# Layer 0 of a four-layer convolution kernel: twelve operations to GpSimd, line sums made once, another set-up order, and the last output by columns

## The chip, the cores and the metric

The kernel runs on one core of a Trainium2 chip. The metric is device time in microseconds, the median of three runs. The core has TensorE (PE, matrix products), VectorE (DVE), ScalarE (ACT) and GpSimd (POOL), and three queues that issue transfers here: SyncE's (SP), ScalarE's and GpSimd's. Each engine and each queue works through its own instructions in order.

## The reference

```python
x = x + L0(gn(x), core0, core1, core2)     # three cores of a tensor train: 16x16x16 -> 16x16x16
x = x + L1(gn(x), ...)                     # depthwise Sobel filters, two dense layers, masks of "alive" cells
x = x + L2(gn(x), filters, bias)           # 3x3 convolution, 16 -> 16 channels
x = x + L3(gn(x), ...)                     # like L1
```

`x` is 1024 x 16 x 16 x 16, float32. `gn` subtracts the mean and divides by the root of the variance of each of 8 groups of 2 channels. The first layer is one linear map of the 4096 values of an image, made of three small cores:

```python
for core in (core0, core1, core2):
    r, o, i, k = core.shape
    new = jnp.einsum('roik,brix->bkox', core, res.reshape(bs, r, i, -1))
```

## The kernel before

**Layer 0.** The batch is two halves of 512 images. The map of layer 0 is done as a fast block multiplication on two levels. The outer table `OUTER` has 13 entries, here called pairs (phases in the code): each names the lines of g that its matrices use (0 to 3), and which blocks of the normalized input its two operands sum. A pair has four units (one for each quarter `q` of the output), and a unit does the seven products of the inner table `INNER`, k = 0 to 6, in 14 steps of 4 matmuls of 128 x 256 (`pieces`, L1567). A 32-bit matmul leaves two records in the trace, so a step is x8 there.

The matrices are built on the fly. `g`, the product of the second and third core, is made by small matmuls (`gmul`, L644), copied by ACT and written to DRAM by `keep_g` in two layouts, `g_dram[0]` (L651) and `g_dram[1]` (L658). `early` makes its first rows (h = 0, q = 0 and 1), on POOL's queue; `piece` makes the rest, woven into the first pair, on SP's queue. `gload` brings two lines of g at a time into a tile `gq`; a third or fourth line goes into a second place (`xn` in the profile). `build` multiplies them on PE (L1459) by `R`, which `coefs` makes from the first core; four ACT copies (L1464) make the result `w`. `mix` adds or subtracts blocks of `w` on DVE: s2, s5, s1, s7, w01 (L1489, L1491). `gather` adds the products to the results on DVE and ACT (L1603 to L1613), with one input in PSUM.

**Opening.** `input_steps` loads the first 512 images in eight transfers on SP's queue. DVE takes their statistics (L1086, L1116), PE transposes the images (L1092), ACT copies them out. `root` and `newton` make the inverse deviation; `widen` and `spread` bring both statistics into the layout of the lines (`mr`), through PE and ACT. `first_normed(b, i)` normalizes a block of the first pair in four DVE operations of 128 x 1024: x00, x11, x10, x01 (L1174). `combined` makes the five operands that the products k >= 2 need (L1203). `kept` stores the raw first rows for later, on POOL's queue. The calls near the end of the program write this order out by hand; `before` lists what is woven in ahead of which step of the first pair. x01 stands ahead of step 7; the sum that needs it stands ahead of step 8, and the product on w01 (k = 5, step 10) reads that sum.

**The second pair's input.** `part_steps(1)` is spread over the first pair. It loads the first block of operand 0 and of operand 1 (two transfers each, L1232), normalizes both on DVE (8 operations each, L1174), saves them to `xb` on SP (L1238), adds block to block (L1242), and then adds from the first pair's blocks (`from_first`, L1315, L1325). The fourth load comes late, since the second unit's results `r` lie in its place until then.

**The third pair** uses the lines (0, 1, 3): `gload` fetches (0, 1) and then (1, 3), and `build` has two groups of matmuls.

**The end.** The last layer's last half of the batch is turned back by `turn`: PE transposes (ptx, L1867), DVE copies into `xo` (L156), which overlies the tile `xn`. Turns come for q = 0 to 3 and w2 = 0 to 7; the last two w2 of q = 3 are done in two half batches `hf`. Ahead of them in the queues stand loads of weights `wq`, of neighbour lines `nx` and of residuals. With (q, w2) = (3, 7) the images leave on SP's queue, in stores of 8 image rows (L1882).

Of the kernel before, what the change touches and what calls it, by code (L numbers as in the profile page):

```python
# [10 lines left out]
F32 = mybir.dt.float32  # L11
# [10 lines left out]
P = 128  # L22
NB = 512
# [82 lines left out]
def conv_preact_kernel(ctx: ExitStack, tc: tile.TileContext, a: dict, out: bass.AP):  # L106
# [97 lines left out]
    al_c = cst("al_c", [P, 2])  # L204
    V.tensor_reduce(al_c, ident.rearrange("p (m v h) -> p v m h", v=2, h=S), AX.XY, ALU.add)
    al_k = cst("al_k", [P, 8])
    KINDS = [(1, 0), (0, 1), (1, 1), (1, -1)]
# [234 lines left out]
    def conv_weights(room):  # L442
# [53 lines left out]
        dram.tile([2, 4, 2, 4, 2, S, 4 * P], F32, tag=f"g_dram{i}", name=f"g_dram{i}") for i in range(2)  # L496
    ]

    xb = {
        (b, n): dram.tile([P, 8, NB], F32, tag=f"xb{b}{n}", name=f"xb{b}{n}")  # L500
        for b in range(4)
        for n in range(NCH)
# [6 lines left out]
            (".... -... .... +...", "+30 +00 -20", "+30")),  # L509
        ((0, 1, 3), None, ("..++ ..++ .... ....", "+30", "+00 -20"),  # L510
            (".-.. .-.. .... .+++", "+10", "+30")),
# [20 lines left out]
    ]  # L532
    UNIT = [(1, 0, 0, 0), (0, 1, 0, 0), (0, 0, 1, 0), (0, 0, 0, 1)]

# [55 lines left out]
    def train_setup(room):  # L590
# [26 lines left out]
        G.memset(room[:, 0:1024], 0.0)  # L617
        for t in range(2):
            V.tensor_copy(c0r[:, t], c0n[:, t].unsqueeze(1).broadcast_to([P, 8, S]))

        def sums():

            t = st0["A"] = work([P, 2, P], "A", "A")
# [23 lines left out]

        def keep_g(h, q, g, queue):

            for w in range(2):  # L650
# [4 lines left out]
            for w in range(2):  # L655
                for v in range(2):
                    rows = slice(64 * w + 32 * v, 64 * w + 32 * v + 32)
                    queue.dma_start(  # L658
                        g_dram[1][v, q, w, :, h].rearrange("o k (t f) -> (k t) o f", t=2), g[rows]
                    )  # L660

        def early():

            g = work([P, 2, 8, P], "w0", "gw")
            pg = [bank([P, 2, 4, 64], "w", "pg") for _ in range(4)]
            for x in range(2):
                for k in range(4):
                    for r in range(4):
                        gmul(pg[r][:, x, k], 0, k % 2, x, r, k // 2)
            for q, x, r in product(range(2), range(2), range(4)):  # L670
                f = 64 * x + 16 * r
                A.copy(
                    g.rearrange("p q (o i) f -> p q i o f", i=2)[:, q, :, :, f : f + S],
                    pg[r][:, x, 2 * q : 2 * q + 2].rearrange("p i (o j) -> p i o j", j=S),
                )
                if (x, r) == (1, 3):
                    keep_g(0, q, g[:, q].rearrange("p (o i) f -> p o (i f)", i=2), G)

        def piece(q, h, r0):
# [13 lines left out]
            if r0 == 2:  # L693
                keep_g(h, q, g.rearrange("p o i f -> p o (i f)"), nc.sync)

        rest = [
# [364 lines left out]
    def input_steps(n, tag, queue):  # L1061
# [108 lines left out]

    def centre_scale(out, x, n, cols, k):

        m = mr[n][:, k, cols].unsqueeze(1).broadcast_to([P, out.shape[1], cols.stop - cols.start])
        V.tensor_tensor(out, out if k else x, m, ALU.mult if k else ALU.subtract)  # L1174

    def first_normed(b, i):

        X, E = part_tile(0)
        cols = slice(256 * i, 256 * i + 256)

        def op(t, k):
            x = X[:, b, t : t + 4, i]
            centre_scale(x, x if b else raw[:, t : t + 4, i], 0, cols, k)

        return [(1.2, lambda t=t, k=k: op(t, k)) for t in (0, 4) for k in range(2)]
# [31 lines left out]
    def part_steps(j):  # L1217
# [15 lines left out]

        def norm(x, n):
            return [(1.2, lambda k=k: centre_scale(x, x, n, full, k)) for k in range(2)]

        def save(block, wh, t, k, x):
            nc.sync.dma_start(xb[block][:, 4 * wh + t : 4 * wh + t + k], x)  # L1238

# [5 lines left out]
        loads = [(0, lambda p=p, wh=wh: load(p, wh)) for p in range(2) for wh in range(2)]  # L1245
        steps = loads[: 3 if j == 1 else 4] + [8]
        for p in range(2):
            if p == 1 and j == 1:
                steps.append(loads[3])
            if first[p] in fresh:  # L1250
                for wh, t in places:
                    steps += norm(lines(p, wh, t, 2), first[p][1])
                    if t:
                        steps.append((0, lambda p=p, wh=wh: save(first[p], wh, 0, 4, lines(p, wh))))
        left = [x[1:] for x in terms]
# [131 lines left out]
    def layer_train():  # L1387
# [34 lines left out]
        def gload(u, h, queue=nc.sync):  # L1422
# [5 lines left out]
            for at in range(0, len(lines), 2):  # L1428
# [6 lines left out]
                if len(pair) == 1:  # L1435
                    pair = (pair[0] - 2, pair[0]) if pair[0] in (2, 3) else (pair[0], pair[0] + 2)
                if pair[1] - pair[0] == 2:
                    queue.dma_start(g, g_dram[0][pair[0], q, h].rearrange("o s k f -> (o s k) f"))
# [35 lines left out]
        def mix(u, what):  # L1474
# [9 lines left out]
            )[what]  # L1484
            into = block(u, 0, 1)
            x, y = block(u, *x), block(u, *y)
            if out:
                t = st[what, u] = work([P, 2, 4, P], out, what)
                V.tensor_tensor(t.rearrange("p s t m -> p (s t m)"), x, y, f)  # L1489
            else:  # L1490
                V.tensor_tensor(into, x, y, f)  # L1491

# [53 lines left out]
        def pieces(u, k):  # L1546
# [176 lines left out]
    def layer_nca(X, n, l, L, xo=None):  # L1723
# [139 lines left out]
        def turn(q, w2, r, hf):  # L1863
# [6 lines left out]
            for v in range(2):  # L1870
# [6 lines left out]
                )  # L1877
            if (q, w2) == (3, 7):
                for h in range(0, S, 8):
                    for g in range(g0, g0 + n):  # L1880
                        b0 = NB + g * P
                        nc.sync.dma_start(  # L1882
                            out[b0 : b0 + P, h : h + 8].rearrange("b h w c -> b (h w c)"),
                            xo[:, g, h : h + 8].rearrange("p h w c -> p (h w c)"),
                        )

# [3 lines left out]

        later = []

# [147 lines left out]
    with ExitStack() as es:  # L2040
# [19 lines left out]
        build(0, 1)  # L2060
        build(0, 0)
        now(stat[1] + tail[:2])
        mix(0, "s2")
        now([spread0] + tail[2:] + [spread1])
        x00, x11, x10, x01 = (first_normed(*at) for at in ((0, 0), (1, 1), (1, 0), (0, 1)))
        now(x00[0::2] + x00[1::2])
        mix(0, "s5")
# [7 lines left out]
            5: more[4:6],  # L2075
            7: x01,
            8: more[6:8],
# [11 lines left out]
        def sums_late(j):  # L2089
            c = combined(j)  # L2090
            woven_into(j, {2 * k + 1: c[2 * k : 2 * k + 2] for k in range(5)})

        late = range(1, NP)
        woven_into(0, before)
# [11 lines left out]
        for i in range(4):  # L2106
# [8 lines left out]
            6: (fold1, 0.92),  # L2115
            7: (set3, 0.85),
            8: (conv_weights(rooms[1]), 0.9),
# [84 lines left out]
```

## Time and profile before

| | us |
|---|---|
| median of three runs (2741.51 to 2749.51) | 2746.04 |
| profiled execution, its own time | 2746.07 |
| its span, first to last instruction | 2744.3 |
| PE busy | 2675.8 (98%) |
| DVE busy | 1994.9 (73%) |
| ACT busy | 1241.4 (45%) |
| POOL busy | 541.3 (20%) |

The first pair's products run from 47 to 183 us of the span, the second pair's from 186 to 313, the third pair's from 313 to 428 (its builds from 295 to 395), and layer 0's last ends near 1560. A line of the profile names the program line, the engine, the operation, the tile written and the tiles read. [...] Buffer numbers are left out of names, so `xn` is either of the two large tiles.

### The profile page before, as it was taken

What the parts mean: (1) busy time and instruction counts of PE and PEld (TensorE: products, weight loads), DVE (VectorE), ACT (ScalarE), POOL (GpSimd) and SP (SyncE); (2) the same over time, 40 slices, a digit from 0 to 9 for tenths busy, and PEclk for the clock granted to TensorE, in tenths of its full rate; (3) what the DMA queues carried; (4) which work ended last, traced back from release to release, by engine and by line L of the source; (5) the groups of instructions that cost most, each with busy time, mean ns of one, the idle gap of its engine ahead of it and who ended that gap; (6) DMA issues with size and microseconds to landing.
All of it is one profiled execution on the core that took longest, in us unless ns stands there. A gap on an engine that the chain in (4) does not pass through costs nothing.

```text
span 2744.3 us, 47734 instructions
## 1 busy us (share of the span) xinstructions
PE 2675.8 (98%) x19246; PEld 1756.9 (64%) x19246; DVE 1994.9 (73%) x2416; ACT 1241.4 (45%) x2091; POOL 541.3 (20%) x690
## 2 busy tenths in 40 slices
PE   6999999999999999999999999999999999999997
PEld 5888888888888878888778733333333333334344
DVE  8597667867787766667887777658778858756654
ACT  3324222222232222333332276776767756676664
POOL 2000351312122742311331111111113221110000
PEclk8999999999999999999999999999999999999998
DMA  7686788997897687889689764555575866444665
GB/s 254 215 317 227 242 169 214 236 221 188 193 242 193 154 187 180 226 229 263 171 188 257 148 165 102 108 159 122 106 195 83 202 150 143 101 89 116 180 175 209
DMA packets 264796, 502.17 MB, mean 183 GB/s; under 512 B 32804, under 2 KB 100440, under 8 KB 255360
## 3 DMA queue, kind: packets, MB, share of 16 engines
q1 hardware_dynamic: 180752, 338.78, 37.1%
q0 software_dynamic: 83632, 160.22, 33.9%
q8 instruction: 152, 2.49, 0.4%
q14 instruction: 68, 0.56, 0.1%
q10 hardware_dynamic: 192, 0.13, 0.0%
HBM read 280.66 MB, written 223.35 MB: 184 GB/s over the span
## 4 chain that ended last, share of the span: by engine, by line
PE 81%; DVE 8%; DMA 5%; issue 3%; POOL 1%; ACT 1%; SPq 0%; DVEq 0%; POOLq 0%; ACTq 0%
PE po L1567 37%; PE ph L1974 21%; PE po L1803 8%; PE po L1658 5%; PE pw L1459 4%; DMA xn<-in_x_dram 1%; PE po L1667 1%; DVE xn L1174 1%; DMA xf<-r 1%; DMA xn<-xf 1%; DVE xn L1203 1%; PE ptx L1867 1%; DMA L_conv_kp<-xn 1%; DMA xb<-xn 0%; DMA xn<-xn 0%
## 5 line engine op out<-in xcount | busy, mean ns | idle before, releaser
L1977 ACT ACTIVATE hid<-ph,pack 128x512 f32<-128x512 f32 (+1 forms) x1040 | 641.3, 684 | 313.5 <-PE ph L1974 254.3
L1567 PE MATMUL po<-xn,s 128*128 128x256 f32 x3328 | 756.7, 384 | 13.6 <-DVE s L1489 7.2
L1567 PEld LDWEIGHTS po<-xn,s 128*128 128x128 f32 x3328 | 628.5, 191 | 117.5 <-issue 16.7
L1567 PE MATMUL po<-xn,w 128*128 128x256 f32 x2496 | 565.0, 381 | 1.4 <-DVE xn L1203 1.4
L1974 PE MATMUL ph<-xn,wq 32*128 32x512 f32 (+1 forms) x3752 | 518.3, 590 | 1.9 <-DVE u L1815 1.5
L1567 PEld LDWEIGHTS po<-xn,w 128*128 128x128 f32 x2496 | 468.2, 190 | 74.1 <-issue 5.9
L1464 ACT COPY w<-pw 128x512 f32<-128x512 f32 x416 | 213.6, 600 | 454.6 <-PE pw L1459 371.8
L1974 PEld LDWEIGHTS ph<-xn,wq 32*128 32x128 f32 x3752 | 233.6, 184 | 228.9 <-issue 210.0
L1974 PE MATMUL ph<-xn,pack 32*128 32x512 f32 x1288 | 274.2, 607 | 5.6 <-DVE u L1815 1.6
L1489 DVE TENSOR_TENSOR s<-w 128x1024 f32<-128x1024 f32 x208 | 251.2, 1217 | 28.1 <-PE po L1567 24.8
L1803 PE MATMUL po<-hid,pack 128*32 128x512 f32 (+1 forms) x2080 | 256.0, 592 | 0.8 <-ACT hid L1977 0.5
L1815 DVE SCALAR_TENSOR_TENSOR u<-po,pack,xn 128x512 f32<-128x512 f32 (+1 forms) x130 | 96.3, 741 | 168.2 <-PE po L1803 167.1
L1857 POOL DMA_DIRECT2D xf<-u x96 | 82.6, 860 | 618.7 <-DVE u L1855 592.1
L754 DVE TENSOR_TENSOR xn<-xn,m 128x1024 f32<-128x1024 f32 x128 | 150.2, 1217 | 34.7 <-ACT m L777 34.6
L1974 PEld LDWEIGHTS ph<-xn,pack 32*128 32x128 f32 x1288 | 115.6, 184 | 90.7 <-issue 63.1
L1803 PEld LDWEIGHTS po<-hid,pack 128*32 128x32 f32 x2080 | 53.9, 109 | 174.9 <-ACT hid L1977 86.3
L1658 PE MATMUL po<-xn,convw 128*128 128x512 f32 x368 | 163.6, 598 | 0.0
L1203 DVE TENSOR_TENSOR xn<-xn 128x1024 f32<-128x1024 f32 x130 | 152.7, 1215 | 8.0 <-DMA L_conv_kp<-xn 8.0
L1459 PE MATMUL pw<-R,gq 32*128 32x128 f32 x3328 | 143.7, 286 | 7.5 <-DVE small L1116 6.9
L1603 DVE TENSOR_TENSOR r<-r,po 128x1024 f32<-128x1024 f32 x78 | 95.0, 1218 | 72.9 <-PE po L1567 61.0
L1459 PEld LDWEIGHTS pw<-R,gq 32*128 32x128 f32 x3328 | 116.2, 188 | 41.9 <-issue 38.6
L1541 POOL DMA_DIRECT2D xf<-xn x69 | 89.8, 1776 | 251.2 <-DVE xn L1534 71.7
(229 smaller groups left out, 2784.9 us busy)
## 6 DMA issues: line engine op xcount, KB each, us to landing
xn<-xf SPq DMA_DIRECT2D x128, 512.0 KB
xn<-xb SPq DMA_DIRECT2D x36, 1024.0 KB
wq<-L_conv_wy SPq DMA_DIRECT2D x192, 192.0 KB
xf<-xn POOLq DMA_DIRECT2D x69, 512.0 KB, 10.8
piece<-xb SPq DMA_DIRECT2D x64, 512.0 KB
xf<-r POOLq DMA_DIRECT2D x48, 512.0 KB, 12.7
xf<-u POOLq DMA_DIRECT2D x96, 256.0 KB, 4.2
gq<-g_dram SPq DMA_DIRECT2D x94, 256.0 KB
```

What stands on the lines that cost most here:

```text
L754: V.tensor_tensor(part, part, m().unsqueeze(1).broadcast_to([P, 2, NB]), op)
L1203: V.tensor_tensor(out, y, z, f)
L1459: T.matmul(pw[r][:, v, i], g[rows, P * (2 * v + i) : P * (2 * v + i) + P], R[rows, k], start=k == 0, stop=k == len(gs) - 1,)
L1464: A.copy(w.rearrange("p b s t m -> p (b s t) m")[:, :, 32 * r : 32 * r + 32].rearrange("p k (v o) -> p v k o", v=2), pw[r].rearrange("p v ...
L1489: V.tensor_tensor(t.rearrange("p s t m -> p (s t m)"), x, y, f)
L1567: T.matmul(po[:, i], matrix(u, what)[:, i, t], x, start=t == 0, stop=t == 3)
L1603: V.tensor_tensor(part, part, po.unsqueeze(2).broadcast_to([P, 2, 2, 256]), ALU.add)
L1658: T.matmul(st["po", h][wh], conv["fw"][:, y], X[:, 16 * wh + h + y - 1], start=y == max(0, 1 - h), stop=y == min(2, S - h),)
L1803: T.matmul(po[32 * j : 32 * j + 32], nca["w1"][:, v], hid[j], start=v == 0, stop=v == 1)
L1815: V.scalar_tensor_tensor(u, po, nca["b1"], X[:, 8 * q + w2, cols(hf)], ALU.add, ALU.add)
L1974: T.matmul(ph, w, x, start=k == 0, stop=k == len(tiles) - 1)
L1977: A.activation(h, ph, AF.Relu, bias=nca["bt"][:, r : r + 1])
```

## The change

Six edits, all in layer 0 but the last two:

- **Set-up order.** The copies `c0r` move into `sums`, and `cores` comes ahead of `sums`; both stand after the first eight statistics. In `early`, the first quarter's writes to `g_dram[0]` are followed by the two loads `gload(0, 1)` and `gload(0, 0)`, and the writes to `g_dram[1]` come after. `build(0, 0)` moves from before the root to after the two `spread` steps. ACT, not DVE, does the widening of the mean (`widen(0)`) of the first half.
- **x01 on GpSimd.** `first_normed(0, 1, G)`: four operations, ahead of the first product in the program's order.
- **Second pair's operand 1 on GpSimd.** `part_steps(1)` takes operand 1 first: its eight normalizations and its two saves go to GpSimd and its queue. The fourth, late load is now the second half of operand 0, so the second unit's results move to column 4096.
- **Sum of two lines of g.** `piece` loads line 0 of each quarter back (tile v0, two loads on SP), DVE adds to line 1 line 0 (`scalar_tensor_tensor` with the 0-or-1 column `low`), and two stores put the sum into `g_sum`. The third pair's entry reads (4, 3), 4 standing for the sum of lines 0 and 1; `gload` takes both from `g_sum` in one load.
- **Layer 3's weights** are set up sooner within their pair (0.75 in place of 0.85).
- **Last output by columns.** With q = 3, `turn` queues columns 0 to 8 at w2 = 3, 8 to 12 at w2 = 5, 12 to 16 at w2 = 7. Each turn sends up to two of them on GpSimd's queue; the last turn sends what is left, its first on SP.

```diff
-        ((0, 1, 3), None, ("..++ ..++ .... ....", "+30", "+00 -20"),
+        ((4, 3), None, ("..++ ..++ .... ....", "+30", "+00 -20"),
...
-        def early():
+        def early(then):
...
                 if (x, r) == (1, 3):
-                    keep_g(0, q, g[:, q].rearrange("p (o i) f -> p o (i f)", i=2), G)
+                    gs = g[:, q].rearrange("p (o i) f -> p o (i f)", i=2)
+                    keep_g(0, q, gs, G, second=False)
+                    if q == 0:
+                        then()
+                        keep_g(0, q, gs, G, first=False)
+            keep_g(0, 1, gs, G, first=False)
...
         def piece(q, h, r0):
+            if h == 1 and r0 == 0:
+                st0["v0"] = t = work([P, 4, 256], "t4", "v0")
+                for w in range(2):
+                    nc.sync.dma_start(
+                        t[64 * w : 64 * w + 64],
+                        g_dram[0][0, q, w].rearrange("o s k (t f) -> (s k t) o f", t=2),
+                    )
...
+            if h == 1 and r0 == 2:
+                t = st0.pop("v0")
+                V.scalar_tensor_tensor(
+                    t, t, low, g.rearrange("p o i f -> p o (i f)"), ALU.mult, ALU.add
+                )
+                for w in range(2):
+                    nc.sync.dma_start(
+                        g_sum[q, w].rearrange("o s k (t f) -> (s k t) o f", t=2),
+                        t[64 * w : 64 * w + 64],
+                    )
...
-                V.tensor_copy(
+                (A.copy if n == k == 0 else V.tensor_copy)(
...
-    def centre_scale(out, x, n, cols, k):
+    def centre_scale(out, x, n, cols, k, on=V):
...
-        V.tensor_tensor(out, out if k else x, m, ALU.mult if k else ALU.subtract)
+        on.tensor_tensor(out, out if k else x, m, ALU.mult if k else ALU.subtract)
...
-        steps = loads[: 3 if j == 1 else 4] + [8]
-        for p in range(2):
-            if p == 1 and j == 1:
-                steps.append(loads[3])
+        steps = ([loads[0]] + loads[2:] if j == 1 else loads) + [8]
+        for p in (1, 0) if j == 1 else (0, 1):
+            on, queue = (G, G) if j == p == 1 else (V, nc.sync)
+            if j == 1 and p == 0:
+                steps.append(loads[1])
...
+                if pair == (4, 3):
+                    queue.dma_start(g, g_sum[q, h].rearrange("o s k f -> (o s k) f"))
...
-                    at = {1: (1, 6144), 3: (1, 14336)}.get(u)
+                    at = {1: (1, 4096), 3: (1, 14336)}.get(u)
...
-            if (q, w2) == (3, 7):
-                for h in range(0, S, 8):
-                    for g in range(g0, g0 + n):
...
+            if q == 3 and w2 in (3, 5, 7):
+                w = slice({3: 0, 5: 8, 7: 12}[w2], 2 * w2 + 2)
+                leave.extend((g, w) for g in range(g0, g0 + n))
+            end = (q, w2, hf) == (3, 7, 1)
+            for i in range(min(len(leave), len(leave) if end else 2)):
+                g, w = leave.pop(0)
+                b0 = NB + g * P
+                (nc.sync if end and i == 0 else G).dma_start(
+                    out[b0 : b0 + P, :, w].rearrange("b h w c -> b h (w c)"),
+                    xo[:, g, :, w].rearrange("p h w c -> p h (w c)"),
+                )
...
-        now([sums])
+        now(stat[0][:1] + [cores, sums])
         coefs(0)
-        now([cores] + stat[0])
-        early()
-        gload(0, 1, queue=G)
-        gload(0, 0, queue=G)
+        now(stat[0][1:])
+        early(lambda: (gload(0, 1, queue=G), gload(0, 0, queue=G)))
...
-        build(0, 0)
         now(stat[1] + tail[:2])
         mix(0, "s2")
-        now([spread0] + tail[2:] + [spread1])
-        x00, x11, x10, x01 = (first_normed(*at) for at in ((0, 0), (1, 1), (1, 0), (0, 1)))
-        now(x00[0::2] + x00[1::2])
+        x00, x11, x10 = (first_normed(*at) for at in ((0, 0), (1, 1), (1, 0)))
+        now([spread0] + tail[2:] + x00[:1] + [spread1])
+        build(0, 0)
+        now(x00[2:3] + x00[1:2] + x00[3:])
+        now(first_normed(0, 1, G))
...
-            7: x01,
...
-            7: (set3, 0.85),
+            7: (set3, 0.75),
```

More of the change, by code (lines that the diff above doesn't have):

```diff
@@ L205, in conv_preact_kernel @@
     V.tensor_reduce(al_c, ident.rearrange("p (m v h) -> p v m h", v=2, h=S), AX.XY, ALU.add)
+    low = cst("low", [P, 1])
     al_k = cst("al_k", [P, 8])
@@ L497, in conv_preact_kernel @@
     ]
+    g_sum = dram.tile([4, 2, 4, 2, S, 4 * P], F32, tag="g_sum", name="g_sum")
     xb = {
@@ L532, in conv_preact_kernel @@
     ]
-    UNIT = [(1, 0, 0, 0), (0, 1, 0, 0), (0, 0, 1, 0), (0, 0, 0, 1)]
+    UNIT = [(1, 0, 0, 0), (0, 1, 0, 0), (0, 0, 1, 0), (0, 0, 0, 1), (1, 1, 0, 0)]
     def read(table):
@@ L617, in train_setup @@
         G.memset(room[:, 0:1024], 0.0)
-        for t in range(2):
-            V.tensor_copy(c0r[:, t], c0n[:, t].unsqueeze(1).broadcast_to([P, 8, S]))
         def sums():
+            for t in range(2):
+                V.tensor_copy(c0r[:, t], c0n[:, t].unsqueeze(1).broadcast_to([P, 8, S]))
             t = st0["A"] = work([P, 2, P], "A", "A")
@@ L646, in gmul, with keep_g @@
             )
-        def keep_g(h, q, g, queue):
-            for w in range(2):
+        def keep_g(h, q, g, queue, first=True, second=True):
+            for w in range(2 * first):
                 queue.dma_start(
@@ L654, in keep_g @@
                 )
-            for w in range(2):
+            for w in range(2 * second):
                 for v in range(2):
@@ L1169, in input_steps, with first_normed @@
         return loads, stat, lines, tail, [lambda: spread(0), lambda: spread(1)], kept
-    def centre_scale(out, x, n, cols, k):
+    def centre_scale(out, x, n, cols, k, on=V):
         m = mr[n][:, k, cols].unsqueeze(1).broadcast_to([P, out.shape[1], cols.stop - cols.start])
-        V.tensor_tensor(out, out if k else x, m, ALU.mult if k else ALU.subtract)
-    def first_normed(b, i):
+        on.tensor_tensor(out, out if k else x, m, ALU.mult if k else ALU.subtract)
+    def first_normed(b, i, on=V):
         X, E = part_tile(0)
@@ L1182, in op @@
             x = X[:, b, t : t + 4, i]
-            centre_scale(x, x if b else raw[:, t : t + 4, i], 0, cols, k)
+            centre_scale(x, x if b else raw[:, t : t + 4, i], 0, cols, k, on)
         return [(1.2, lambda t=t, k=k: op(t, k)) for t in (0, 4) for k in range(2)]
@@ L1232, in load, with norm, save @@
             nc.sync.dma_start(lines(p, wh), source(first[p], first[p] in fresh, wh, 0, 4))
[L1234 to L1238, printed above, removed]
+        def norm(x, n, on=V):
+            return [(1.2, lambda k=k: centre_scale(x, x, n, full, k, on)) for k in range(2)]
+        def save(block, wh, t, k, x, queue=nc.sync):
+            queue.dma_start(xb[block][:, 4 * wh + t : 4 * wh + t + k], x)
         def add(p, wh, t, x, sign):
@@ L1245, in part_steps @@
         loads = [(0, lambda p=p, wh=wh: load(p, wh)) for p in range(2) for wh in range(2)]
-        steps = loads[: 3 if j == 1 else 4] + [8]
-        for p in range(2):
-            if p == 1 and j == 1:
-                steps.append(loads[3])
+        steps = ([loads[0]] + loads[2:] if j == 1 else loads) + [8]
[3 more added lines that the diff above has]
+                steps.append(loads[1])
             if first[p] in fresh:
                 for wh, t in places:
-                    steps += norm(lines(p, wh, t, 2), first[p][1])
+                    steps += norm(lines(p, wh, t, 2), first[p][1], on)
                     if t:
-                        steps.append((0, lambda p=p, wh=wh: save(first[p], wh, 0, 4, lines(p, wh))))
+                        steps.append((0, lambda p=p, wh=wh, queue=queue: save(
+                            first[p], wh, 0, 4, lines(p, wh), queue
+                        )))
         left = [x[1:] for x in terms]
@@ L1436, in gload @@
                     pair = (pair[0] - 2, pair[0]) if pair[0] in (2, 3) else (pair[0], pair[0] + 2)
-                if pair[1] - pair[0] == 2:
+                if pair == (4, 3):
+                    queue.dma_start(g, g_sum[q, h].rearrange("o s k f -> (o s k) f"))
+                elif pair[1] - pair[0] == 2:
                     queue.dma_start(g, g_dram[0][pair[0], q, h].rearrange("o s k f -> (o s k) f"))
@@ L1484, in mix @@
             )[what]
-            into = block(u, 0, 1)
             x, y = block(u, *x), block(u, *y)
@@ L1490, in mix @@
             else:
-                V.tensor_tensor(into, x, y, f)
+                V.tensor_tensor(block(u, 0, 1), x, y, f)
         def matrix(u, what):
@@ L1877, in turn @@
                 )
-            if (q, w2) == (3, 7):
-                for h in range(0, S, 8):
-                    for g in range(g0, g0 + n):
[L1881 to L1891, printed above, removed]
+            if q == 3 and w2 in (3, 5, 7):
[9 more added lines that the diff above has]
+                )
+        later, leave = [], []
         def after(n, fn):
@@ L2091, in sums_late @@
             woven_into(j, {2 * k + 1: c[2 * k : 2 * k + 2] for k in range(5)})
+        V.tensor_reduce(low, ident.rearrange("p (w v r) -> p v w r", w=2, v=2)[:, 0], AX.XY, ALU.add)
         late = range(1, NP)
```

## The prediction

> **What bounds the kernel now.** I read the page first: PE is busy 98% of the span, and only the first slice (6 tenths) and the last (7) stand out. So a saving counts only where PE idles, or if PE itself gets less work. The timeline of the engines (start, duration, engine, line, operation, count; in brackets the idle time before it and what ended that) then shows the places the change touches.
>
> The opening, PE:
>
> ```profile
> 33.67 2.09 PE L1459 MATMUL pw<-R,gq 32*128 32x128 f32 x32 [6.89 <-DVE small L1116]
> ...
> 47.14 3.78 PE L1567 MATMUL po<-xn,s 128*128 128x256 f32 x8 [2.63 <-DVE xn L1174]
> ...
> 77.38 1.99 PE L1567 MATMUL po<-xn,w 128*128 128x256 f32 x8 [1.36 <-DVE xn L1203]
> ```
>
> The first build really waits for its operand, not for DVE: the load of gq goes out on POOL at 29.03 and takes 4.5 us. The first product starts at 47.14; from there DVE runs one 1.14 us operation after another, but PE lacks work only once more, for 1.36 us. So from 47 to 77 us PE and DVE are nearly level.
>
> The one long PE wait after the opening, at the first product of the second pair, and the two groups of a build for the third:
>
> ```profile
> 185.75 8.83 PE L1567 MATMUL po<-xn,s 128*128 128x256 f32 x32 [2.80 <-DVE s L1489]
> ...
> 295.06 0.50 PE L1459 MATMUL pw<-R,gq 32*128 32x128 f32 x8
> 295.39 0.40 PE L1459 MATMUL pw<-R,xn 32*128 32x128 f32 x8
> ```
>
> A build with a second group has twice the matmuls; PE is 100% busy there. At 185.75 PE came late because DVE had been full since about 135.
>
> The end, SP's queue and DVE:
>
> ```profile
> 2721.34 11.27 SPq L1882 DMA_DIRECT2D out_dram<-xn  x8
> ...
> 2727.80 0.58 DVE L156 COPY xn<-ptx 128x128 f32<-128x128 f32 x2 [0.53 <-PE ptx L1867]
> ```
>
> Eight stores of 1 MB all leave after 2721; the last evacuation ends at 2728.4, the span at 2744.3. 8.4 MB at about 420 GB/s is 20 us: the tail is a transfer.
>
> [...] (DVE and POOL at the same time):
>
> ```profile
> 325.25 2.34 DVE L1203 TENSOR_TENSOR xn<-xn 128x1024 f32<-128x1024 f32 x2
> ...
> 325.78 11.29 POOL L279 TENSOR_SCALAR_AFFINE_SELECT xn<-xn 48x256 f32<-48x256 f32 x6
> ```
>
> These selects take 0.39 us when free and up to 4.78 us here; each ended 0.33 us into a DVE operation with one input in PSUM (L1603, L1613) or in a DVE gap. DVE kept its 1.136 us pace. So back-to-back DVE starves POOL, and POOL enters at a gap; a longer POOL operation would then hold DVE up. [...] (512 B in 27 ns, 8192 B in 309 ns), but 4096 B packets made of 512 B runs on the POOL queue take 159 ns, no slower than contiguous ones.
>
> **The change, part by part.** The sum is made against the profiled execution: 2746.07 us, span 2744.3; the median of three runs, 2746.04, is the same.
>
> *Opening.* The copies of the first core now stand behind the first eight statistics (2.65 us from 9.1), so their transposes come at 12.1, and the 64 small products (3.69 us), which PE holds behind them, at 12.8 instead of 9.71: 3 us lost. The first writes of g leave POOL at 18.3 instead of 15.17. Against that, the loads of gq wait for these two alone, not for ten more DMAs on the queue. The second of them landed about 9.8 us after its issue (25.64 less 15.8), so the load leaves at 28.2 and lands, at 4.2, at 32.4; the build starts 1.1 earlier, its copies end 4.17 later (37.84 less 33.67), at 36.8. The root is no longer behind the second build's copies: newton (1.29) ends at 39.2, widen and the transposes (0.65, 1.1, 0.6) give the second statistic at 41.6; the first, by four ACT copies of about 0.2, at 39.7. Two subtractions wait for the one, two products for the other, and PE starts at 43.2: **3.9 earlier** (0 if the writes land late, 5.5 if they land as early as now).
>
> DVE loses the four operations of x01 (4.6 us)[...]. Without interference PE runs on at once and gains 3.9 + 1.36 = 5.3. With it, POOL gets in at the wait for the first statistic (or not), at the wait for s5 (its build now comes after the transposes: copies until 45.2)[...]. DVE's list to the third product is 4 + 1 + 10 operations, the wait and `low`: 58.0 if free, 61.5 to 63.9 with two or three entries. From the third product to 77.38 less 1.36 there are now 14.8 us of PE work, so PE would be there at 76.3 to 78.7, and 1.7 later where the idle turned the clock down ([...] the 32 matmuls at 185.75 took 8.83 against 7.17 before). That is -1 to +3. I take **-0.5** for the opening, with -5.3 and +3 as ends: the interference eats the gain.
>
> *Second pair.* Eight normalizations (9.1 us) leave DVE[...], with two stores behind them on its queue; nothing else is due there before 181. They start when their lines land, about 124, and are needed by the additions at 158.5 (L1242). DVE is half idle until 135, so most get in there; the last few enter at PSUM operations[...]. The other eight take the place of the moved ones, so DVE is as full as before from 141 on, and gains four additions of `v0` (1.2 each, two after 135). The load that DVE waited 1.95 for at 149.3 no longer stands behind a store on SP (L1238). The g_sum detour puts 8 small loads and 8 small stores, 4 MB, on SP where the DMA engines are 98% busy; SP waits there for DVE, and the xr stores and line loads behind it with it. Ends: -2 (the load's wait gone, POOL harmless) and +6 ([...] the loads late). I take **+1.5**.
>
> *Third pair.* Eight builds lose the second group. A build of both lasts 2.00 (295.06 to 297.06), of one 1.10: **-7.2** (ends -6.5, -8). PE has no wait there that would take its place. 8 loads of 256 KB and two coefficient operations go too, beside PE.
>
> *End.* Eleven of twelve stores leave on POOL's queue, two to a turn, from about 2703: 2 MB then, 2 MB at 2710, 1 MB each at 2714, 2717 and 2722. POOL had nothing there. At 400 GB/s each batch ends before the next. After the last evacuation there are two stores of 0.5 MB in 256 B runs, one on SP and one on POOL. Issue: 256 runs take POOL 0.63 and 128 take 0.56, so 2048 runs some 2 to 3; then about 1 to the first byte, 1.3 (packed) to 2.3 (an estimate of 18 ns a run from the packet records) of data: 2734 to 2735.5 where the last data now lands at 2742.4. The 1.9 from there to the end stays. Upper end: POOL's short runs at 230 GB/s back up, or make wq and nx loads late: 3 gained. I take **-7.5** (ends -9, -3).
>
> *Nothing:* ACT's widening (ACT is idle in the opening), the place of the second unit's sums, L3's weights sooner in their pair (DVE 80% busy, PE without waits there).
>
> **Sum:** -0.5 + 1.5 - 7.2 - 7.5 = -13.7, **2732.4 us**.
>
> **Rivals.** (1) *POOL does not hold DVE* (it uses only what DVE leaves): opening -5.3, second pair -2: -22, 2724. For: DVE's pace beside the selects was unharmed. Against: those needed 0.33 us, inside a 1.13 us operation[...]. (2) *The stores are not hidden*: descriptors of 2048 runs and 256 B rows, tail -3, second pair +4: -6.7, 2739.4. For: no DMA of this form is in the trace. Against: POOL's packed 512 B runs. (3) *Slower:* POOL is starved in the second pair. If it enters only at DVE's PSUM operations, five per unit of 28 us, eight need 45 us from 124: the lines are ready near 170, not 158.5. DVE waits 12 where it is full until the second pair starts, and PE waits those 12 more there; with opening +3, SP +4 and half-clock windows 3, that is +22 - 14.7: 2753. It decides if DVE is backlogged when the lines land; DVE's 16.8 of 20 us busy in 120 to 140, eight moved operations among it, speak against. (4) That the sums are not used is excluded by the order of the built program: 128 matmuls fewer.
>
> **Numbers.** Forecast 50%, rival 1 26%, rival 2 15%, rival 3 9%. No change, as this kernel can be measured, is within 0.3%, 8.2 us. Rival 1 and nearly all of the forecast's range (2725 to 2739) is faster, rival 2 is mostly same: faster 0.75, same 0.16, slower 0.09. The range takes in rivals 1 and 2 and the bounds: 2722 to 2742.
>
> **What would show it.** Right: first product near 43 and no gain left by the product on `w` (near 77); [...] DVE operations after a gap stretched too; no L1459 with xn in the third pair; 6 to 9 us from the last evacuation to the end, with stores from 2703. Wrong: DVE at an even 1.14 through the opening (rival 1), stores still running 12 us after the last evacuation (2), PE waiting over 10 us at the first product of the second pair (3).

## The result and the profile after

The changed kernel takes **2752.89 us** (median of 14 runs; before on the same chip 2745.53). The ratio is 1.0028, 95% interval 1.0018 to 1.0038: 7.4 us slower by the medians where 13.7 faster was forecast, and above the range given. The profiled execution has a span of 2750.8 us (before 2744.3).

Where it is lost and found, from the starts of the same products in the two traces:

| stretch of the span | forecast | measured |
|---|---|---|
| opening: start of the second unit, 86.94 to 90.95 | -0.5 | +4.0 |
| from there to the second pair's first product, 185.75 to 199.08 | +1.5 | +9.3 |
| from there to the end of the third pair's products, 428.68 to 435.69 | -7.2 | -6.3 |
| the pair that sets up layer 3's weights and its neighbours, 1096.66 to 1099.78 | 0 | -3.9 |
| last evacuation to the end of the span, 15.9 to 19.4 | -7.5 | +3.4 |

The rest, up to the last evacuation, changes by -0.1. The fourth row is mostly chance, as E4 shows. The timeline of PE in the opening of the changed kernel (start, duration, engine, line, operation, count; in brackets the idle time before and what ended it):

```profile
30.92 1.56 PE L1488 MATMUL pw<-R,gq 32*128 32x128 f32 x32 [3.96 <-DVE small L1140]
...
45.92 3.78 PE L1595 MATMUL po<-xn,s 128*128 128x256 f32 x8 [2.04 <-DVE xn L1198]
...
63.33 6.55 PE L1595 MATMUL po<-xn,w 128*128 128x256 f32 x16 [3.25 <-DVE xn L1227]
...
80.94 1.25 PE L1595 MATMUL po<-xn,w 128*128 128x256 f32 x5
```

The build starts 2.75 us sooner (33.67 before), but the first product only 1.2. PE then waits 3.25 for an operand, and runs the next 16 matmuls at little more than half the pace: 6.55 us at a granted clock of 0.56 of full speed, where the kernel before had no wait, a clock of 1.00 and 3.62 us:

```profile
61.19 3.62 PE L1567 MATMUL po<-xn,w 128*128 128x256 f32 x16
```

The product on w01, foretold for 76.3 to 78.7, or 1.7 later behind a slow clock, starts at 80.94 (before 77.38).

GpSimd and DVE over the same stretch, from their timelines:

```profile
37.23 2.35 POOL L1198 TENSOR_TENSOR xn<-xn 128x1024 f32<-128x1024 f32 x1
41.90 9.46 POOL L1198 TENSOR_TENSOR xn<-xn 128x1024 f32<-128x1024 f32 x3 [2.31 <-ACT xn L1167]
```
```profile
36.70 2.94 DVE L1152 TENSOR_TENSOR small<-small 128x32 f32<-128x32 f32 x1
39.67 0.63 DVE L1158 COPY wide<-small 128x128 f32<-128x128 f32 x4
40.22 8.92 DVE L1198 TENSOR_TENSOR xn<-xn 128x1024 f32<-128x1024 f32 x4
49.07 3.37 DVE L1517 TENSOR_TENSOR s<-w 128x1024 f32<-128x1024 f32 x1
```

The same two groups on DVE in the kernel before:

```profile
43.60 4.62 DVE L1174 TENSOR_TENSOR xn<-xn 128x1024 f32<-128x1024 f32 x4
48.14 1.22 DVE L1489 TENSOR_TENSOR s<-w 128x1024 f32<-128x1024 f32 x1
```

A GpSimd operation takes 2.35 alone and 3.15 (9.46 / 3) beside DVE; the four of DVE take 8.92 instead of 4.62, one s 3.37 instead of 1.22, and even a tiny operation of 0.19 takes 2.94. From 41.9 to 52.4 us, where both have 128 x 1024 operations, the two engines **take turns**, one whole operation each: those of GpSimd start at 41.90, 44.74 and 48.14, those of DVE at 42.49, 45.79 and 49.07, each of DVE's 3.36 or 3.37 long.

In the second pair's preparation, DVE and GpSimd again:

```profile
138.41 2.11 DVE L711 SCALAR_TENSOR_TENSOR v<-v,low,xn 128x1024 f32<-128x1024 f32 x1 [9.91 <-DMA g_dram<-xn]
140.45 3.36 DVE L1562 SCALAR_TENSOR_TENSOR neg<-xn 128x1024 f32<-128x1024 f32 x1
143.74 6.65 DVE L1517 TENSOR_TENSOR s<-w 128x1024 f32<-128x1024 f32 x2
150.31 1.21 DVE L1631 TENSOR_TENSOR r<-r,po 128x1024 f32<-128x1024 f32 x1
```
```profile
132.36 10.37 POOL L1198 TENSOR_TENSOR xn<-xn,xn 128x1024 f32<-128x1024 f32 x4 [81.01 <-DMA xn<-xr]
...
143.63 12.27 POOL L1198 TENSOR_TENSOR xn<-xn,xn 128x1024 f32<-128x1024 f32 x4
```

DVE stands 9.91 us at the second addition of v0, with `neg` and the two s behind it in its order, and comes out of it into GpSimd's turns. Of the lines shown, only the operation that reads one input from PSUM (`po`, at 150.31) keeps its 1.21 us beside a GpSimd addition. The line of the wait names a store of g. The addition needs no store; it needs the line of g, which was there when its own store left SP at 130.89, and the load of v0, which left SP only at 127.49, behind three line loads of 1 MB:

```profile
120.99 5.60 SPq L1256 DMA_DIRECT2D xn<-xr  x3
127.10 0.34 SPq L1467 DMA_DIRECT2D gq<-g_dram  x1
127.49 1.29 SPq L690 DMA_DIRECT2D v<-g_dram  x2
130.89 1.25 SPq L653 DMA_DIRECT2D g_dram<-xn  x2
```

The long wait of PE ahead of the second pair's first product grew from 2.80 to 4.18 (the profile names nothing that ended it), and there is a new one of 4.13 ahead of it, in the first pair, behind which 16 matmuls take 5.61 instead of 3.72:

```profile
147.16 5.61 PE L1595 MATMUL po<-xn,s 128*128 128x256 f32 x16 [4.13 <-DVE s L1517]
...
199.08 8.69 PE L1595 MATMUL po<-xn,s 128*128 128x256 f32 x32 [4.18 <-issue]
```

The end, GpSimd's and SP's queue (the last evacuation ends at 2731.4, the span at 2750.8):

```profile
2706.69 4.63 POOL L1913 DMA_DIRECT2D out_dram<-xn  x4 [229.66 <-DVE xn L156]
2717.85 4.53 POOL L1913 DMA_DIRECT2D out_dram<-xn  x4 [6.54 <-DVE u L1843]
2724.76 2.26 POOL L1913 DMA_DIRECT2D out_dram<-xn  x2 [2.37 <-DVE xn L156]
2731.84 1.11 POOL L1913 DMA_DIRECT2D out_dram<-xn  x1 [4.82 <-DVE xn L156]
```

A line of GpSimd's here is its time for the issue alone: 4.63 us for the four stores of 1 MB, which took 12.8 each to land (median). The stores leave early, as forecast. But the packets of GpSimd's queue move about 260 KB/us while the runs are 512 B (packets of 4096 B in about 235 ns) and about 180 when they are 256 B (306 ns), against 420 for the stores of before. The queue does not drain (the DMA engines are 95% busy from 2709 to 2748); what it holds at the last evacuation takes 19 us.

### The profile page after: what moved, and what is told of

It reads as the page before. It is cut to its first block, busy times and chain, and to the rows that moved or that the text cites. A ratio compares the mean times of both kernels' runs of the same rounds, so it can differ in the third digit from the quotient of the medians.

```text
span 2750.8 us, 47258 instructions
## 1 busy us (share of the span) xinstructions
PE 2668.7 (97%) x18990; PEld 1749.2 (64%) x18990; DVE 2003.4 (73%) x2403; ACT 1241.5 (45%) x2095; POOL 577.9 (21%) x715
## 4 chain that ended last, share of the span: by engine, by line
PE 86%; DVE 8%; DMA 3%; issue 1%; ACT 1%; SPq 0%; POOL 0%; POOLq 0%; DVEq 0%
PE po L1595 43%; PE ph L2005 21%; PE po L1831 8%; PE po L1686 5%; PE pw L1488 4%; PE po L1695 1%; DVE xn L1198 1%; PE ptin L1116 1%; DMA xn<-xf 1%; DVE bn L1110 1%; PE ptx L1895 1%; DVE s L1517 1%; DMA xn<-xr 1%; DVE u L1843 0%; DMA xn<-in_L_conv_fc_w_dram 0%
## 5 line engine op out<-in xcount | busy, mean ns | idle before, releaser
L1517 DVE TENSOR_TENSOR s<-w 128x1024 f32<-128x1024 f32 x208 | 258.0, 1250 | 26.2 <-PE po L1595 25.8
```

## The experiments

Every kernel was timed beside the kernel before (2743.5 to 2744.3 median in the four groups); "ratio" is to that, with its 95% interval. The table gives the start of a product in each kernel's trace less that in the kernel before, and the end of the span. Units are counted from the first one of layer 0, four to a pair.

| kernel | unit 1 (47.14) | unit 2 (86.94) | unit 5, second pair (185.75) | unit 13, fourth pair (428.68) | last evacuation to end (15.9) | span (2744.3) |
|---|---|---|---|---|---|---|
| changed kernel | -1.2 | +4.0 | +13.3 | +7.0 | 19.4 | +6.5 |
| E1 output by columns alone | -0.2 | -0.2 | -0.1 | -0.4 | 18.7 | +6.6 |
| E2 sum alone | -0.5 | -0.3 | +8.9 | +2.7 | 15.9 | -2.2 |
| E3 GpSimd's twelve alone | +3.9 | +7.5 | +10.8 | +10.7 | 16.0 | +9.7 |
| E4 layer 3's weights alone | -0.3 | +1.4 | +1.3 | +1.3 | 16.0 | -0.8 |
| E5 set-up order alone | -5.9 | +3.1 | +3.3 | +3.0 | 15.7 | -1.7 |
| E6 sum, v0 sooner | -0.2 | +1.2 | +5.9 | -1.2 | 16.1 | -1.8 |
| E7 columns, all on SP | 0.0 | 0.0 | 0.0 | -0.3 | 11.7 | -1.5 |
| E8 set-up order, E6, E4 | -5.5 | +3.2 | +7.9 | +1.6 | 16.2 | -1.6 |
| E9 set-up, kept(1) first | -5.5 | -4.7 | -4.7 | -4.9 | 15.9 | -8.1 |
| E10 columns in two halves | -0.4 | +1.3 | +1.2 | +1.7 | 11.3 | -8.1 |
| E11 parts that pay | -5.4 | -4.1 | +1.4 | -5.5 | 10.9 | -12.0 |
| E12 changed, without GpSimd's twelve | -5.7 | +3.3 | +13.4 | +6.5 | 19.4 | +6.0 |
| E13 E11 with GpSimd's twelve | -1.2 | +2.9 | +11.4 | +7.0 | 11.6 | +0.2 |

The span of one execution also carries a wait that has nothing to do with most of these edits, see E4; so single parts are judged by the stretch they touch and by the interval of the times. The starts vary too: E4 and E10 edit nothing ahead of the second unit and start it 1.4 and 1.3 late, so differences of that size are not an edit's.

### GpSimd's operations alone (E3)

The kernel before, with only these of the change:

```diff
-            7: x01,
+        now(first_normed(0, 1, G))      # ahead of mix(0, "s5")
...
+            on, queue = (G, G) if j == p == 1 else (V, nc.sync)
```

> The kernel before with the twelve operations on GpSimd alone (four of x01 in the opening, eight normalizations of the second pair with their order and their stores); no sum, set-up as before. Theory T (DVE and GpSimd take turns): each GpSimd operation takes about 3.1 where DVE is busy, and DVE's two-input operations about double; the product on w near 79 to 81 instead of 77.38; DVE's room is too small before the second pair, whose first product starts 2 to 5 us later; with the sum taken away the time is 2 to 4 us longer than before. Rival G (it alone makes the loss of the first pair): the second pair 10 to 13 us later and the time 8 to 12 us longer. Rival F (GpSimd uses only what DVE leaves): the second pair 2 to 5 us sooner, the time 2 to 5 us shorter.

Measured: ratio 1.0038 (1.0026 to 1.0050), some 10 us slower. The operations take turns as theory T says, but the loss has rival G's size: +7.5 at the second unit, +10.8 at the second pair. The timeline of DVE in this kernel shows it without any other edit:

```profile
45.31 8.92 DVE L1175 TENSOR_TENSOR xn<-xn 128x1024 f32<-128x1024 f32 x4
54.15 3.37 DVE L1492 TENSOR_TENSOR s<-w 128x1024 f32<-128x1024 f32 x1
```

Three entries of GpSimd cost DVE 4.3 + 2.15, so 2.1 each, and one ahead of them as much (an operation of 0.19 takes 2.30); an operation moved away saves DVE 1.14. Where DVE is the later engine, moving one costs about 1 us.

That alone does not explain the 10.8, which is not spread evenly: the four operations of x01 make 7.5 of it, the eight of the second pair 3.3. What differs is the place. The four turns all lie ahead of the third product, which starts at 68.29 where the kernel before has 61.19, 7.1 later. The 4.6 us that DVE is spared come only at step 7, and from there on PE had only one wait of 1.36 to give back. The eight fall in part on time in which DVE waits for PE anyway (2.21 and 1.59 us between 133 and 144). No run has x01 on GpSimd at a later place, so what such a place would cost is open.

### The sum alone, and with an earlier load (E2, E6)

E2 has the table entry (4, 3), v0, `low` and `g_sum` in the kernel before. E6 loads v0 of lines 1 to 3 behind the preceding sum's store:

```diff
-            if h == 1 and r0 == 0:
-                st0["v0"] = t = work([P, 4, 256], "t4", "v0")   # and its two loads
+            if (q, h, r0) == (0, 1, 0):
+                fetch(0)                                        # the same, for quarter 0
...
+                if q < 3:
+                    fetch(q + 1)                                # behind the stores to g_sum
```

> The kernel before with the sum of two lines alone; all normalizations stay on DVE. Theory W (DVE waits in order for the load of v0): DVE stands 6 to 10 us at the addition of v0 (about 138), the first product of the second pair starts 5 to 10 us later than 185.75, the builds of the third pair give 6 to 7 us back; the time within 3 us of before. Rival G (the loss of the first pair is GpSimd's twelve operations): no such stand, the first product of the second pair within 2 us of 185.75, and the time about 7 us shorter than before.

> The kernel with the sum of two lines alone (as in the run of that part), and v0 of lines 1 to 3 loaded one piece sooner, ahead of the 1 MB loads on SP. Theory W (the loss is DVE's wait for that load): the wait of 7.6 us at 134 is gone or under 1 us, the fifth unit starts 1 to 4 us after the 185.75 of before (instead of 8.9), and the time is 3 to 6 us shorter than before. Rival D (four more additions and 4 MB more on SP cost it wherever they stand): the second pair 6 us or more late again, the time that of before within 1 us.

E2: ratio 1.0011 (1.0003 to 1.0019). The wait is there without a single operation on GpSimd, and the second pair comes 8.9 later; the builds then give 6.2 back. In E6 the same addition (timelines of DVE, E2 and E6):

```profile
134.46 1.28 DVE L707 SCALAR_TENSOR_TENSOR v<-v,low,xn 128x1024 f32<-128x1024 f32 x1 [7.63 <-DMA g_dram<-xn]
```
```profile
128.64 1.23 DVE L1200 TENSOR_TENSOR xn<-xn,xn 128x1024 f32<-128x1024 f32 x1 [2.91 <-DMA xn<-xr]
129.78 1.28 DVE L711 SCALAR_TENSOR_TENSOR v<-v,low,xn 128x1024 f32<-128x1024 f32 x1
```

The stores of g are the same in both, so the load of v0 was the cause. Theory W is right on the wait and wrong on the size: the fifth unit is still 5.9 late (4.6 of it after the second unit, 9.3 in E2), near rival D's 6. DVE has four more additions and now waits 2.91 and 2.45 for line loads, which stand behind the loads of v0; that these make the 4.6 is argued, not shown. The ratio is 0.9991 (0.9983 to 1.0000).

### The set-up's order alone, and with one store sooner (E5, E9)

E5 is the new order of the set-up in the kernel before. E9 adds this:

```diff
-        kept(0)
-        kept(1)
+        kept(1)
+        kept(0)
```

> The kernel before with the set-up's new order alone (statistics ahead of the first core, loads of gq ahead of the other writes, second build behind the root, ACT's widening); x01 and all normalizations on DVE. Theory T (what the opening lost is the turns of DVE and GpSimd): the first product starts at 43 to 44 instead of 47.14 and the gain holds to the second unit, which starts 3 to 5 us sooner than 86.94; time 3 to 4 us shorter. Rival (DVE is full in the opening whatever the order): the first product 3 us sooner, but the second unit within 1 us of before, since DVE has four operations of x01 to do again; the same time.

> The kernel before with the set-up's new order, and the store of the half that x11 overwrites (kept(1)) issued on GpSimd's queue ahead of the other 2 MB (kept(0)) instead of behind them. Theory K (the order's gain of 5.9 us at the first product was lost at 52.4, where DVE waited 8.1 us for that store to have read): the wait is under 2 us, the first product at 41 to 42, the second unit starts 3 to 5 us sooner than 86.94, and the time is 3 to 5 us shorter than before. Rival (DVE is full up to the second unit and the wait stood in for work): the second unit within 1 us of before, the same time.

E5 started at 41.25, sooner than either theory said, and was still 3.1 late at the second unit: ratio 1.0010 (1.0003 to 1.0018). Both theories fell. The timeline of DVE in E5 names what neither had:

```profile
43.03 1.23 DVE L1496 TENSOR_TENSOR s<-w 128x1024 f32<-128x1024 f32 x1 [0.78 <-ACT w L1472]
52.38 9.67 DVE L1179 TENSOR_TENSOR xn<-xn 128x1024 f32<-128x1024 f32 x8 [8.12 <-DMA xr<-xn]
```

x11 writes over the images in place, and must wait until `kept(1)` has read them. That store is the last of three on GpSimd's queue and leaves it 3 us later than before, because the ten writes of g ahead of it now stand behind the loads of gq (GpSimd's queue, before and E5):

```profile
33.34 0.89 POOL L1148 DMA_DIRECT2D xr<-xn  x1
```
```profile
36.41 0.89 POOL L1153 DMA_DIRECT2D xr<-xn  x1
```

And DVE comes at 44.2, 5 us sooner than before (49.27, with no wait). E9's DVE:

```profile
43.42 1.22 DVE L1496 TENSOR_TENSOR s<-w 128x1024 f32<-128x1024 f32 x1 [0.75 <-ACT w L1472]
44.56 9.66 DVE L1179 TENSOR_TENSOR xn<-xn 128x1024 f32<-128x1024 f32 x8
```

The wait is gone, as theory K says, the second unit starts 4.7 sooner, and 4.9 is left at the fourth pair: ratio 0.9981 (0.9971 to 0.9990), some 5 us faster.

### The output by columns (E1, E7, E10)

E1 is that part alone in the kernel before. E7 and E10 alter it so:

```diff
-                (nc.sync if end and i == 0 else G).dma_start(
+                nc.sync.dma_start(                                 # E7
...
-            if q == 3 and w2 in (3, 5, 7):
-                w = slice({3: 0, 5: 8, 7: 12}[w2], 2 * w2 + 2)
+            if q == 3 and w2 in (3, 7):                            # E10
+                w = slice(2 * w2 - 6, 2 * w2 + 2)
...
+                (G if w.start == 0 else nc.sync).dma_start(        # E10
```

> The kernel before with the stores of the last output by columns alone. Theory R (the rate of short runs): the stores move 512 B and 256 B runs at about 260 and 175 KB/us, so their queue never drains; from the last evacuation to the end of the span 19 to 20 us instead of 15.9, the time 3 to 4 us longer than before. Rival Q (the forecast as it stood): the stores drain behind the work and only the last 0.5 MB shows; about 8 us from the last evacuation to the end, 7.5 us shorter than before. Rival N (the late end of the changed kernel came from something else in it, such as the weights or the late start of everything): no difference within 1 us.

> The kernel before with the output by columns, all twelve stores on SP's queue instead of GpSimd's. Theory R (the length of the runs sets the rate): packets of 256 B take about 17 ns and of 512 B about 27 ns, so 8.4 MB take 32 us of data with nothing between; from the last evacuation to the end 16 to 19 us, the time within 2 us of the run of that part on GpSimd's queue. Rival P (GpSimd's queue is the slow part): 8 to 10 us from the last evacuation to the end, the time 5 us or more shorter than before, unless SP's loads of nx behind the stores come late and make PE wait before 2728.

> The kernel before with the last output in two halves of eight columns, all runs 512 B: the first half on GpSimd's queue from 2707, the second on SP's, where no load stands behind it. Theory R (the end is set by bytes at the rate of their runs, and by what waits behind them on the queue): 4.2 MB at 260 KB/us on GpSimd are through by 2724, the second half lands 14 to 16 us after its first issue at 2725; 9 to 11 us from the last evacuation to the end instead of 15.9, PE without a new wait, the time 5 to 7 us shorter than before. Rival (the engines share one rate of about 200 KB/us whatever the queue): 16 to 20 us from the last evacuation to the end, no gain.

E1: ratio 1.0009 (1.0000 to 1.0018); 18.7 from the last evacuation to the end, so the part itself loses 2.7. E7 brings 11.7, which looks like a gain half way to rival P, but the last evacuation from which it counts is itself late. Against the start of layer 0's last pair, E7's end is 2.1 sooner than E1's and 0.9 later than before, so theory R is nearer. A store of 512 B runs moves about 280 KB/us on SP's queue (27 ns a packet), one of 256 B runs 212 (16 ns), both more than on GpSimd's. But the first stores now stand ahead of weight loads on SP, and PE waits for one (timeline of PE in E7):

```profile
2710.91 4.12 PE L1980 MATMUL ph<-xn,wq 32*128 32x256 f32 x38 [4.27 <-DMA wq<-L_conv_wy]
```

So the last evacuation is 5.2 later against the start of that pair (+2.8 against -2.4), and the time is that of before: ratio 0.9998 (0.9988 to 1.0008). E10 has no 256 B runs, and nothing waits behind its stores (queues of E10):

```profile
2700.03 4.62 POOL L1888 DMA_DIRECT2D out_dram<-xn  x4 [229.98 <-DVE xn L156]
```
```profile
2717.71 11.36 SPq L1888 DMA_DIRECT2D out_dram<-xn  x4
```

The end comes 11.3 after the last evacuation: 4.7 gained, and the times say the same, a little under the 5 to 7 of theory R: ratio 0.9983 (0.9975 to 0.9990). Both the length of the runs and, less, the queue set the rate; the theory that the run alone does was too simple.

### Layer 3's weights (E4)

```diff
-            7: (set3, 0.85),
+            7: (set3, 0.75),
```

> The kernel before with the weights of L3 at 0.75 of their pair instead of 0.85 alone. Theory S (the kept and packed copies leave POOL about 11 us sooner, and DVE no longer waits 8 us for them at 1003): PE's waits at 995 to 1014, 4.3 us together, are gone; the time 3 to 5 us shorter than before. Rival (the forecast as it stood): the same time within 1 us, since the waits come from elsewhere.

Ratio 1.0002 (0.9994 to 1.0010). The kernel before has a wait of DVE in this pair, which the changed kernel has not (timeline of DVE, before):

```profile
989.08 1.21 DVE L1203 TENSOR_TENSOR xn<-xn 128x1024 f32<-128x1024 f32 x1
998.30 1.23 DVE L1203 TENSOR_TENSOR xn<-xn 128x1024 f32<-128x1024 f32 x1 [8.01 <-DMA L_conv_kp<-xn]
```

With 0.85, in nine kernels' traces, the pair takes 108.9 to 118.8, mean 111.9: the wait has another length each time. With 0.75, in six, it takes 108.9 every time, and the pair before it takes 111.7 instead of 110.15. On average 1.4 us are gained. So theory S has the mechanism, but the 3.9 of the two traces compared above was a large draw; the times cannot tell 1.4 from nothing.

### Parts together (E8, E11, E12, E13)

E8: set-up order, E6's sum, layer 3 at 0.75. E11: the same with `kept(1)` first and E10's output. E12: the changed kernel with x01 and the eight normalizations back on DVE, in the order of before. E13: E11 with the twelve operations on GpSimd as in the changed kernel.

> The set-up's order, the sum with v0 loaded one piece sooner, and the weights of L3 at 0.75, without GpSimd's twelve operations and with the stores of before. If the parts add up (set-up -3.5, sum -4, L3 0 to -4 by how long the kernel before waits there): 6 to 10 us shorter than before. Rival (what is gained ahead of the second pair is lost to DVE, full until then): no more than 4 us shorter.

> The set-up's order with the store of the overwritten half first, the sum with v0 loaded one piece sooner, L3's weights at 0.75, and the last output in two halves of eight columns; nothing on GpSimd's ALU. If the parts add up: set-up -4, sum -1 to -2, L3 0 to -3, tail -6: 10 to 14 us shorter than before. Rival (the second pair's line loads, 2.5 to 4 us of DVE's time, take the set-up's gain): 6 to 8 us shorter.

> The changed kernel with the twelve operations back on DVE, with the order and place that they had before; everything else of the change stays. Theory O (the turns of DVE and GpSimd fall into the two waits, for kept(1) at 52 and for v0 at 134, and cost little beside them): the fifth unit starts at 196 to 199 (set-up alone +3.3, sum alone +8.9 on 185.75) instead of 199.08, the time 0 to 3 us shorter than the changed kernel's. Rival G (the twelve operations cost as much as alone, 10.8 us): the fifth unit at 188 to 190, the time 8 to 10 us shorter than the changed kernel's, as fast as before or faster.

> The kernel of the parts that pay (set-up's order with kept(1) first, v0 sooner, L3's weights, output in two halves) with the twelve operations on GpSimd again. Theory T (DVE and GpSimd take turns, so a GpSimd addition of 3.1 takes about as much from DVE as it saves it): without the waits to hide in, the twelve cost 4 to 10 us; the time that much longer than the kernel of the parts that pay. Rival (the moved operations relieve DVE, full before the second pair, once the waits are gone): 2 to 4 us shorter than that kernel.

E8: ratio 1.0003 (0.9994 to 1.0013), the rival's side; its set-up still had the wait for `kept(1)`. **E11: 2734.1 us median of 6 runs, ratio 0.9955 (0.9937 to 0.9972)**, some 12 us faster than before by the ratio, 9.4 by the medians, and 19 faster than the changed kernel. Most of that is the order of the stores and the output in halves: at the fourth pair E11 has -5.5 where E9 alone has -4.9, and its end is 5.0 shorter. The sum adds little there. The same product as above, timeline of PE, E12:

```profile
199.10 1.26 PE L1595 MATMUL po<-xn,s 128*128 128x256 f32 x3 [4.45 <-DVE s L1517]
```

It is at 199.10 where the changed kernel has 199.08, and the ratio to before is 1.0028 in both (E12: 1.0018 to 1.0037). Inside the whole change the twelve operations cost nothing, though alone they cost 10.8. E12's DVE waits for `kept(1)` and for v0, and this time the profile names that load:

```profile
52.43 2.49 DVE L1198 TENSOR_TENSOR xn<-xn 128x1024 f32<-128x1024 f32 x2 [8.02 <-DMA xr<-xn]
...
139.02 1.28 DVE L711 SCALAR_TENSOR_TENSOR v<-v,low,xn 128x1024 f32<-128x1024 f32 x1 [7.94 <-DMA v<-g_dram]
```

In the changed kernel the turns filled much the same time: its DVE comes to x11 at 52.36, after the turns and without a wait. E13 takes those waits away and leaves the turns: 2745.93 us, 11.8 more than E11's median and 11.0 more when each is taken against the kernel before beside it. At the second pair it is +10.0 (+11.4 against +1.4), and again the four of x01 make most of that: +7.0 at the second unit. Theory T is right, somewhat above its own upper end of 10.

## Why the prediction was wrong, step by step

- **Opening, "the interference eats the gain".** Its sum was -0.5, its ends -5.3 and +3; measured +4.0. Three steps failed.
  - The first is "back-to-back DVE starves POOL, and POOL enters at a gap", and with it "two or three entries". I had read it off the 0.39 us selects, which did wait, up to 4.78 us, while DVE went on. The additions of E3 do not stand back like that: the two engines alternate, one whole operation each, and neither side wins. GpSimd got in after each DVE operation while it had work, four times, at 2.1 us each for DVE. Why the selects waited and the additions did not, no run shows. The third product still came at 63.33, inside the 61.5 to 63.9 of the prediction. That was luck: without turns the new order is 2 us faster than the "58.0 if free" (56.00 in E11), and the turns cost 7.3 where 3.5 to 5.9 were allowed. What an entry would cost was my estimate; no trace of before has such an addition on GpSimd. It took 2.35 alone.
  - The second is PE's pace behind its wait, priced at 1.7 at most: the 16 matmuls lost 2.9. The granted clock stood at half from 62.27 to 69.10, 6.83 us, at a wait of 3.25. The 1.7 came from the product at 185.75 in the kernel before, where it stood at half for 3.41 us, from 186.49 to 189.90, at a wait of 2.80. With the 2.9 the prediction's own sum from the third product, 63.33 + 14.8 + 2.9 = 81.0, meets the measured 80.94 for the product on w01.
  - The third is "the loads of gq wait for these two alone". It counted what the new order moved ahead, and not what it moved back by 3 us: the store of `kept(1)`, for which x11 waits. E5 has the better start (41.25, not 43.2) and the 8.1 us wait; in the changed kernel the turns hid it.
- **Second pair, +1.5.** The term for the sum held four additions and the traffic, and said "SP waits there for DVE". It was the other way round: DVE waited for a load that SP had issued behind 3 MB. E2 shows 8.9 for this term alone, and E6 that the sooner load takes back about half; the eight operations on GpSimd added nothing here (E12). The forecast that the moved normalizations start at 124 was 8 us early (132.36), and they met a DVE that came backlogged out of its wait. My third rival had a slower kernel at this product by POOL being starved; the sign was right, the mechanism was not: PE waited 4.18, not over 10, and POOL was done at 155.9. That the rival's time of 2753 is the measured one is chance.
- **Third pair, -7.2.** Right in mechanism; measured -6.3, in E2 -6.2 and in E6 -7.1. The 128 matmuls with the second group are gone (4352 to 4096 records of builds).
- **End, -7.5.** Measured +3.4. The step that failed is "At 400 GB/s each batch ends before the next". It rested on one row of packets of 512 B runs on POOL's queue (159 ns); here such packets took 235, those of 256 B runs 306. With 260 and 180 KB/us the same arithmetic leaves the queue full. E10 shows that 4.7 were to be had.
- **Layer 3's weights, nothing.** I wrote "PE without waits there" and had overlooked PE's waits of 0.79, 2.53, 0.36 and 0.64 at 995 to 1014, behind DVE's wait. Over many traces it is worth 1.4, hidden by how much that wait varies.
- **Rival 2** (stores not hidden) came nearest at the end, with the wrong price: -3 there, +3.4 measured.

## What to carry to other kernels

Before an operation is moved to GpSimd, price what it takes from DVE, not what it takes on GpSimd: in E3, where both did 128 x 1024 operations in SBUF and DVE had no idle time, DVE lost 2.1 us for each 1.14 us operation that it was spared. Ask also when: DVE loses the time where GpSimd does the work, and gets it back where it would have done the work itself. In the opening the loss came ahead of a product that PE was waiting for, and the gain behind it. When a queue's order is changed, list what is moved back too, and for each transfer that gives a buffer free or fills one, ask which in-order engine stands at it next; both 8 us waits here (8.12 in E5, 7.63 in E2) were of that kind, and moving one store or one load took each away. Two waits at the same place hide each other, so undo one part in the full change and also try each part alone before blaming it.

## What the runs showed of the hardware that was not expected

- GpSimd's 128 x 1024 additions alternate with DVE's whole operations: 3.15 us each against 2.35 alone, 3.37 for DVE's against 1.22, and a DVE operation of 0.19 us took 2.94 when it met one. A DVE operation with one input in PSUM was not held up (1.21 us at 150.31, beside a GpSimd addition).
- PE's granted clock fell to half at a wait of 2.80 us (186.49 to 189.90 in the kernel before, 3.41 us) and at one of 3.25 us (62.27 to 69.10 in the changed one, 6.83 us).
- Stores from SBUF to DRAM in short runs, alone on their queue: 512 B runs about 260 KB/us on GpSimd's queue and 280 on SP's, 256 B runs about 180 and 212; 8 KB runs 420.
- A tail of some 40 us of queued stores did not slow the work beside it in E1: from layer 0's last pair to the last evacuation it lost 0.3 us. Only order on a queue did, in E7: a wait of PE of 4.27 us for weights.
